# Pairwise bilinear products: two-tile loads of x from GpSimd in 16 KB rows, and W without its last zeros

## The chip, the cores and the metric

The kernel runs on one core of a Trainium2 chip. The metric is the device time of one launch in microseconds (us), lower is better. Before the change it was 1322.44 us, the median of 3 runs from 1320.73 to 1324.12. Everything is in 32-bit floats.

## The reference

For 4096 samples with 32 fields of 64 values each, every pair of fields i < j (496 pairs) has a matrix of its own. Field i is multiplied by the matrix, and the result elementwise by field j:

```python
i_idx, j_idx = np.triu_indices(32, k=1)        # 496 pairs
vi = inputs[:, i_idx, :]                       # (4096, 496, 64)
vj = inputs[:, j_idx, :]
vdotw = jnp.einsum('bpd,pde->bpe', vi, W)      # W: (496, 64, 64)
inter = vdotw * vj
return inter.reshape(4096, -1)                 # (4096, 31744)
```

The output has 520 MB, x (the inputs) 33.6 MB and W 8 MB. Nearly all that is moved is output.

## The kernel before

The samples are cut into 32 tiles of 128, one sample to a partition; a tile of x is 128 rows of 8 KB. For each tile TensorE transposes x in two halves, ScalarE copies the transposes to SBUF, TensorE multiplies them by W, and VectorE multiplies the products by x into a ring in SBUF. From the ring the tile goes out in four stores of 128 rows (30,208, 26,112, 31,488 and 39,168 bytes a row). The ring holds 28,160 columns, less than the 31,744 of a tile, so VectorE has to wait for stores. The first half of a tile's transposes is done within the last store group of the tile before it.

x has three slots in SBUF, and is loaded in the list that this function makes: load 0 is tile 0, load i is tiles 2i-1 and 2i in two slots side by side, and the last is tile 31 alone. Tile 2i-1 is always in slot 1; a load is written in the program at the start of tile 2i-2, and slot 1 is free when tile 2i-3 is done.

```python
DMA_ENGINES = 16
LIGHT = 4
LIGHT_TILES = [4, 6, 8, 10, 12, 14, 18, 20, 22, 24, 26, 28, 30]
PAIRS_FROM = [6, 8, 10, 12, 14, 0, 1]
HEAD = P // DMA_ENGINES        # 8
REST = HEAD // 2               # 4
PAD = 16

def x_slots(NT):
    loads = [[(0, 0)]]
    for t in range(1, NT, 2):
        if t + 1 == NT:
            loads.append([(t, 1)])
        elif loads[-1][-1] == (t - 1, 2):
            loads.append([(t + 1, 0), (t, 1)])
        else:
            loads.append([(t, 1), (t + 1, 2)])
    return loads
```

Most transfers are spread evenly over the 16 DMA engines, 8 rows to each. For some tiles GpSimd issues the load so that one engine (LIGHT) gets no rows of it: 120 rows go as 15 blocks of 8 rows to the 15 engines after it, and the other 8 rows as 2 blocks of 4 to two of the engines in the list PAIRS_FROM. The design rests on a cursor that moves round the engines with each DMA of GpSimd's; where it doesn't stand at the wanted engine, a small DMA of a few bytes (a nudge) moves it there. The blocks lie in DRAM with 16 elements of padding between them, so that a block stays a block.

```python
    def from_engine(e):
        nonlocal cursor
        k = (e - cursor) % DMA_ENGINES
        if k:
            nudge = nudges[e == LIGHT + 1]
            from_pool(
                nudge[:k].rearrange("p (h c) -> p h c", h=2)[:, :, :4],
                x[: k * 8].rearrange("(p h c) -> p h c", p=k, h=2),
            )
        cursor = e

    def load_beside(at, xt, lap):
        nonlocal cursor
        most = DMA_ENGINES - 1
        for e, k, rows, p in (
            (PAIRS_FROM[lap % len(PAIRS_FROM)], 2, REST, most * HEAD),
            (LIGHT + 1, most, HEAD, 0),
        ):
            from_engine(e)
            n = rows * F * D
            blocks = x[at : at + k * (n + PAD)].rearrange("(k c) -> k c", k=k)
            from_pool(xt[p : p + k * rows], blocks[:, :n])
            at += k * (n + PAD)
            cursor = (e + k) % DMA_ENGINES

    def load_x(load):
        at = sum(x_sizes[: x_loads.index(load)])
        parts = [[(t, s)] for t, s in load] if any(t in LIGHT_TILES for t, s in load) else [load]
        for part in parts:
            t, s = part[0]
            n = len(part) * F * D
            if t in LIGHT_TILES:
                load_beside(at, slot[t], LIGHT_TILES.index(t))
            else:
                nc.scalar.dma_start(
                    out=xbuf[:, s * F * D : s * F * D + n],
                    in_=x[at : at + P * n].rearrange("(p c) -> p c", p=P),
                )
            at += sum(tile_sizes[t] for t, s in part)
```

So 13 tiles come from GpSimd, 15 tiles singly from ScalarE's queue, and two loads (tiles 1 and 2, tiles 15 and 16) as pairs from ScalarE's queue in rows of 16 KB.

W lies in SBUF as 128 partitions: the upper 64 hold the matrices of even fields, the lower 64 those of odd ones. The odd fields have fewer pairs, so the lower half ends in 960 columns of zeros. W comes in five loads:

```python
    for g in LOADS:
        upto = woff[2 * g[-1]] + width[2 * g[-1]]
        nc.sync.dma_start(out=w_sb[:, done:upto], in_=w[:, done:upto])
        done = upto
```

Of the kernel before, what the change touches and what calls it, by code (L numbers as in the profile page):

```python
# [12 lines left out]
P = 128  # L13
# [10 lines left out]

DMA_ENGINES = 16
LIGHT = 4
LIGHT_TILES = [4, 6, 8, 10, 12, 14, 18, 20, 22, 24, 26, 28, 30]
PAIRS_FROM = [6, 8, 10, 12, 14, 0, 1]
HEAD = P // DMA_ENGINES
REST = HEAD // 2  # L30
PAD = 16
# [14 lines that stand above are left out]
# [3 lines left out]
def pair_bilinear_kernel(  # L49
# [32 lines left out]
    nc = tc.nc  # L82
    NT = out.shape[1] * 2 // (F * (F - 1) * D)
    NPR = F // 2

    width = [(F - 1 - i) * D for i in range(F)]
# [4 lines left out]
    woff = [i % 2 * D + sum(width[i % 2 : i : 2]) for i in range(F)]  # L91
# [13 lines left out]
    xbuf = const.tile([P, 3 * F * D], F32, tag="x", name="x")  # L105
    x_loads = x_slots(NT)
    pads = (DMA_ENGINES + 1) * PAD
    tile_sizes = [P * F * D + (pads if t in LIGHT_TILES else 0) for t in range(NT)]
    x_sizes = [sum(tile_sizes[t] for t, s in load) for load in x_loads]
    slot = {t: xbuf[:, ts(s, F * D)] for load in x_loads for t, s in load}  # L110

    nudges = [const.tile([DMA_ENGINES, 16], F32, tag=f"nudge{i}", name=f"nudge{i}") for i in range(2)]
# [2 lines left out]
    def from_pool(out, in_):  # L115

        tc.keep_in_program_order(nc.gpsimd.dma_start(out=out, in_=in_))  # L117

    def from_engine(e):

        nonlocal cursor
        k = (e - cursor) % DMA_ENGINES
        if k:
            nudge = nudges[e == LIGHT + 1]
            from_pool(
                nudge[:k].rearrange("p (h c) -> p h c", h=2)[:, :, :4],
                x[: k * 8].rearrange("(p h c) -> p h c", p=k, h=2),
            )
        cursor = e

    def load_beside(at, xt, lap):

        nonlocal cursor
        most = DMA_ENGINES - 1
        for e, k, rows, p in (
            (PAIRS_FROM[lap % len(PAIRS_FROM)], 2, REST, most * HEAD),
            (LIGHT + 1, most, HEAD, 0),
        ):
            from_engine(e)
            n = rows * F * D  # L140
            blocks = x[at : at + k * (n + PAD)].rearrange("(k c) -> k c", k=k)
            from_pool(xt[p : p + k * rows], blocks[:, :n])
            at += k * (n + PAD)
            cursor = (e + k) % DMA_ENGINES

    def load_x(load):

        at = sum(x_sizes[: x_loads.index(load)])
        parts = [[(t, s)] for t, s in load] if any(t in LIGHT_TILES for t, s in load) else [load]
        for part in parts:  # L150
            t, s = part[0]
            n = len(part) * F * D
            if t in LIGHT_TILES:
                load_beside(at, slot[t], LIGHT_TILES.index(t))
            else:
                nc.scalar.dma_start(
                    out=xbuf[:, s * F * D : s * F * D + n],
                    in_=x[at : at + P * n].rearrange("(p c) -> p c", p=P),
                )
            at += sum(tile_sizes[t] for t, s in part)  # L160

    pring = psum.tile([P, BANKS * BANK], F32, tag="pring", name="pring")
    bank = 0
# [21 lines left out]
    at = 0  # L185

    load_x(x_loads[0])
    w_sb = const.tile([P, sum(width[0::2])], F32, tag="w", name="w")
    done = 0
    for g in LOADS:  # L190

        upto = woff[2 * g[-1]] + width[2 * g[-1]]
        nc.sync.dma_start(out=w_sb[:, done:upto], in_=w[:, done:upto])
        done = upto

    transpose_x(slot[0], 0)
    for t in range(NT):
        xt = slot[t]
        for load in x_loads:
            if min(load)[0] == t + 1:  # L200
                load_x(load)
        for s, group in enumerate(STORES):
            if at + store_w[s] > RING:
                at = 0
# [3 lines left out]
            for p in group:  # L208
# [5 lines left out]
                for c1 in range(first, width[2 * p] + 1, BANK):  # L214
                    n = first if c1 == first else BANK
                    c0 = c1 - n
                    odd = width[2 * p + 1] and c1 > D
# [28 lines left out]
                out=out[:, t * cols + o0 : t * cols + o0 + store_w[s]], in_=osb  # L246
# [49 lines left out]
```

## Time and profile before

The profiled execution took 1321.16 us, with a span of 1319.0 us from its first to its last instruction and a mean granted TensorE clock of 0.970.

| | before |
|---|---|
| time, median of 3 | 1322.44 us |
| moved by DMA | 562.90 MB, mean 427 GB/s |
| HBM read, written | 41.95 MB, 520.09 MB |
| DMA packets | 25404 |
| store of 4896 KB, issue to landing | 17.7 us |
| x from ScalarE, 1024 KB, issue to landing | 18.7 us |
| x from GpSimd, 960 KB, issue to landing | 26.4 us |

Engines are TensorE (PE, and PEld for its weight loads), VectorE (DVE), ScalarE (ACT), GpSimd (POOL) and SyncE (SP), which issues the loads of W and the stores. A row of the queue table has packets, megabytes and the share of 16 engines' span that the packets took. q1 is SyncE's queue, q10 ScalarE's, q0 GpSimd's, q8 fetches instructions. A line such as "DVE ring L231 <- DMA out_dram<-ring" reads: VectorE at line 231, which writes the ring, waited for a store of the ring to DRAM; then the total in us, how often, and the longest wait. L181 is the transpose, L182 its copy, L221 the matmul, L231 and L239 VectorE's products, L156 ScalarE's load of x and L117 every DMA of GpSimd's. The table of stretches has, for each stretch of the span, the busy time of each engine, then the granted clock, the share of the 16 DMA engines' time that was busy (a packet is counted where it starts, so a short stretch can have over 1), and GB/s.

### The profile page before, as it was taken

What the parts mean: (1) busy time and instruction counts of PE and PEld (TensorE: products, weight loads), DVE (VectorE), ACT (ScalarE), POOL (GpSimd) and SP (SyncE); (2) the same over time, 40 slices, a digit from 0 to 9 for tenths busy, and PEclk for the clock granted to TensorE, in tenths of its full rate; (3) what the DMA queues carried; (4) which work ended last, traced back from release to release, by engine and by line L of the source; (5) the groups of instructions that cost most, each with busy time, mean ns of one, the idle gap of its engine ahead of it and who ended that gap; (6) DMA issues with size and microseconds to landing.
All of it is one profiled execution on the core that took longest, in us unless ns stands there. A gap on an engine that the chain in (4) does not pass through costs nothing.

```text
span 1319.0 us, 13176 instructions
## 1 busy us (share of the span) xinstructions
PE 1159.3 (88%) x5376; PEld 534.3 (41%) x5376; DVE 1182.1 (90%) x1376; ACT 66.1 (5%) x65; POOL 30.2 (2%) x58
## 2 busy tenths in 40 slices
PE   6998889889898998998999889888998989899893
PEld 3443344343444443443344444334443344344441
DVE  5998899989899998998999899889998989899894
ACT  1000000000000000000000000000000000000000
POOL 0000000000000000000000000000000000000000
PEclk9999999999999998998999989999999999999997
DMA  9999999999999999999999999999999999999998
GB/s 393 430 431 433 425 432 430 432 431 427 427 427 429 430 429 429 430 429 434 429 428 427 430 431 424 431 426 428 428 432 429 421 429 421 428 430 434 430 431 378
DMA packets 25404, 562.90 MB, mean 427 GB/s; under 512 B 4480, under 2 KB 4480, under 8 KB 4736
## 3 DMA queue, kind: packets, MB, share of 16 engines
q1 hardware_dynamic: 19152, 528.49, 93.5%
q10 hardware_dynamic: 2448, 19.92, 3.6%
q0 software_dynamic: 3744, 13.65, 2.5%
q8 instruction: 42, 0.69, 0.2%
q14 instruction: 18, 0.15, 0.0%
HBM read 41.95 MB, written 520.09 MB: 426 GB/s over the span
## 4 chain that ended last, share of the span: by engine, by line
DMA 50%; DVE 35%; issue 8%; PE 6%; DVEq 0%; ACT 0%
DMA out_dram<-ring 49%; DVE ring L231 30%; PE pring L221 6%; DVE ring L239 5%; DMA x<-in_x_dram 1%; DVEq L231 0%; PE pring L181 0%; ACT xT L182 0%; DVEq L292 0%; DVEq L239 0%
## 5 line engine op out<-in xcount | busy, mean ns | idle before, releaser
L221 PE MATMUL pring<-w,xT 64*128 64x512 f32 (+4 forms) x4864 | 1096.2, 561 | 132.1 <-DVE ring L231 111.1
L231 DVE TENSOR_TENSOR ring<-pring,x 128x1024 f32<-128x1024 f32 (+3 forms) x1056 | 1103.5, 1105 | 106.1 <-DMA out_dram<-ring 77.8
L221 PEld LDWEIGHTS pring<-w,xT 64*128 64x128 f32 x4864 | 478.8, 190 | 708.8 <-DVE ring L231 519.7
L182 ACT COPY xT<-pring 128x1024 f32<-128x1024 f32 x64 | 64.8, 1012 | 1208.9 <-PE pring L181 1208.9
L239 DVE TENSOR_TENSOR ring<-pring,x 128x64 f32<-128x64 f32 (+3 forms) x320 | 97.1, 352 | 13.6 <-DMA out_dram<-ring 13.6
L181 PEld LDWEIGHTS pring<-ident,x 128*128 128x128 f32 x512 | 55.5, 142 | 56.7 <-DVE ring L231 48.2
L181 PE MATMUL pring<-ident,x 128*128 128x128 f32 x512 | 70.8, 282 | 8.6 <-DMA x<-in_x_dram 8.5
L117 POOL DMA_DIRECT2D x<-in_x_dram x26 | 15.2, 585 | 1076.3 <-DVE ring L239 1076.1
L117 POOL DMA_DIRECT2D nudge<-in_x_dram x26 | 14.5, 559 | 0.3 <-issue 0.3
L182 ACT ACT_TABLE_LOAD x1 | 1.3, 1283 | 1.7 <-PEq L288 1.7
masks.py:199 POOL TENSOR_SCALAR_AFFINE_SELECT ident<-ident 128x128 f32<-128x128 f32 x1 | 0.3, 287 | 0.1
masks.py:197 POOL MEMSET ident<- 128x128 f32 x1 | 0.2, 204 | 0.3 <-POOLq L288 0.3
L288 POOL MEMSET const-float32-0.0<- 128x1 f32 x1 | 0.1, 98 | 0.2 <-issue 0.2
L288 POOL MEMSET const-bfloat16-1.0<- 128x1 bf16 x1 | 0.1, 101 | 0.0
L288 POOL MEMSET const-uint8-127<- 128x1 uint8 x1 | 0.1, 101 | 0.0
L288 POOL MEMSET const-float32-1.0<- 128x1 f32 x1 | 0.1, 98 | 0.0
## 6 DMA issues: line engine op xcount, KB each, us to landing
out_dram<-ring SPq DMA_DIRECT2D x32, 4896.0 KB, 17.7
out_dram<-ring SPq DMA_DIRECT2D x32, 3936.0 KB, 17.7
out_dram<-ring SPq DMA_DIRECT2D x32, 3776.0 KB, 19.7
out_dram<-ring SPq DMA_DIRECT2D x32, 3264.0 KB, 20.1
x<-in_x_dram ACTq DMA_DIRECT2D x15, 1024.0 KB, 18.7
x<-in_x_dram POOLq DMA_DIRECT2D x13, 960.0 KB, 26.4
x<-in_x_dram ACTq DMA_DIRECT2D x2, 2048.0 KB, 18.2
w<-in_w_dram SPq DMA_DIRECT2D x1, 2592.0 KB, 28.2
```

Source lines behind the costliest of these rows:

```text
L117: tc.keep_in_program_order(nc.gpsimd.dma_start(out=out, in_=in_))
L181: nc.tensor.transpose(pt[:, ts(c, P)], xt[:, ts(n * g + c, P)], ident)
L182: nc.scalar.copy(xT[:, ts(g, 2 * BANK)], pt)
L221: nc.tensor.matmul(pm[:, h * BANK : h * BANK + n], xT[h * D : (h + 1) * D, ts(p, P)], w_sb[h * D : (h + 1) * D, a : a + n], start=True, st ...
L231: nc.vector.tensor_tensor(runs(osb, o[0], o[1], n), runs(pm, 0, BANK, n), bass.AP(xj.tensor, xj.offset, [xj.ap[0], [0, 2], xj.ap[1]]), ALU ...
L239: nc.vector.tensor_tensor(osb[:, o[h] + h * D : o[h] + n], pm[:, h * (BANK + D) : h * BANK + n], xj[:, h * D :], ALU.mult,)
L288: nc = bacc.Bacc("TRN2", target_bir_lowering=False, num_devices=1)
```

## The change

GpSimd now brings whole loads of two tiles, in rows of 16 KB: six of them, loads 3, 5, 8, 10, 13 and 15 (tiles 5 and 6, 9 and 10, 15 and 16, 19 and 20, 25 and 26, 29 and 30). Twelve tiles instead of thirteen thus leave out the LIGHT engine. All other pairs come from ScalarE as one DMA of 16 KB rows. The last load of W is split into the columns in which both halves have data, and the last 960 columns of the upper half alone; the zeros are no longer moved. PAIRS_FROM is longer and starts elsewhere, and a nudge by one engine gets a form of its own, which doesn't occur with these lists. The aim is fewer and longer packets, fewer nudges and completions, less to move, and small blocks spread over more engines.

```diff
-LIGHT_TILES = [4, 6, 8, 10, 12, 14, 18, 20, 22, 24, 26, 28, 30]
-PAIRS_FROM = [6, 8, 10, 12, 14, 0, 1]
+LIGHT_LOADS = [3, 5, 8, 10, 13, 15]
+PAIRS_FROM = [5, 7, 9, 11, 13, 15, 1, 2, 0, 14, 12, 10, 8, 6]
 ...
-    def load_beside(at, xt, lap):
+    def load_beside(at, xt, n_row, lap):
 ...
-            n = rows * F * D
+            n = rows * n_row
 ...
     def load_x(load):
-        at = sum(x_sizes[: x_loads.index(load)])
-        parts = [[(t, s)] for t, s in load] if any(t in LIGHT_TILES for t, s in load) else [load]
-        for part in parts:
-            ... (each tile of a pair by itself, as above)
+        i = x_loads.index(load)
+        at = sum(x_sizes[:i])
+        n = len(load) * F * D
+        s = load[0][1]
+        xt = xbuf[:, s * F * D : s * F * D + n]
+        if i in LIGHT_LOADS:
+            load_beside(at, xt, n, LIGHT_LOADS.index(i))
+        else:
+            nc.scalar.dma_start(out=xt, in_=x[at : at + P * n].rearrange("(p c) -> p c", p=P))
 ...
         upto = woff[2 * g[-1]] + width[2 * g[-1]]
-        nc.sync.dma_start(out=w_sb[:, done:upto], in_=w[:, done:upto])
+        odd = woff[F - 1] + width[F - 1]
+        both = min(upto, odd)
+        nc.sync.dma_start(out=w_sb[:, done:both], in_=w[:, done:both])
+        if both < upto:
+            nc.sync.dma_start(out=w_sb[:D, both:upto], in_=w[:D, both:upto])
         done = upto
```

The order of x in DRAM is prepared to match: the rows of a GpSimd load hold both its tiles.

More of the change, by code (lines that the diff above doesn't have):

```diff
@@ L107, in pair_bilinear_kernel @@
     pads = (DMA_ENGINES + 1) * PAD
-    tile_sizes = [P * F * D + (pads if t in LIGHT_TILES else 0) for t in range(NT)]
-    x_sizes = [sum(tile_sizes[t] for t, s in load) for load in x_loads]
+    x_sizes = [
+        P * len(load) * F * D + (pads if i in LIGHT_LOADS else 0) for i, load in enumerate(x_loads)
+    ]
     slot = {t: xbuf[:, ts(s, F * D)] for load in x_loads for t, s in load}
@@ L124, in from_engine @@
             nudge = nudges[e == LIGHT + 1]
[L125 to L128, printed above, removed]
+            if k == 1:
+                from_pool(nudge[:3, :8], x[:64].rearrange("(g c) -> g c", g=2)[:, :12])
+            else:
+                from_pool(
+                    nudge[:k].rearrange("p (h c) -> p h c", h=2)[:, :, :4],
+                    x[: k * 8].rearrange("(p h c) -> p h c", p=k, h=2),
+                )
         cursor = e
-    def load_beside(at, xt, lap):
+    def load_beside(at, xt, n_row, lap):
         nonlocal cursor
@@ L146, in load_x @@
     def load_x(load):
-        at = sum(x_sizes[: x_loads.index(load)])
-        parts = [[(t, s)] for t, s in load] if any(t in LIGHT_TILES for t, s in load) else [load]
-        for part in parts:
[L151 to L160, printed above, removed]
+        i = x_loads.index(load)
[5 more added lines that the diff above has]
+            load_beside(at, xt, n, LIGHT_LOADS.index(i))
+        else:
+            nc.scalar.dma_start(out=xt, in_=x[at : at + P * n].rearrange("(p c) -> p c", p=P))
     pring = psum.tile([P, BANKS * BANK], F32, tag="pring", name="pring")
@@ L261 @@
     x = []
-    for load in x_slots(NT):
-        tiles = [t for t, _ in load]
-        if not any(t in LIGHT_TILES for t in tiles):
-            x.append(rows[:, tiles].ravel())
-            continue
-        for t in tiles:
-            if t in LIGHT_TILES:
-                k = (DMA_ENGINES - 1) * HEAD
-                for part in (
-                    rows[k:, t].reshape(2, REST * F * D),
-                    rows[:k, t].reshape(DMA_ENGINES - 1, HEAD * F * D),
-                ):
-                    x.append(np.pad(part, ((0, 0), (0, PAD))).ravel())
-            else:
-                x.append(rows[:, t].ravel())
+    for i, load in enumerate(x_slots(NT)):
+        of_load = rows[:, [t for t, _ in load]]
+        if i in LIGHT_LOADS:
+            k = (DMA_ENGINES - 1) * HEAD
+            for part in (of_load[k:].reshape(2, -1), of_load[:k].reshape(DMA_ENGINES - 1, -1)):
+                x.append(np.pad(part, ((0, 0), (0, PAD))).ravel())
+        else:
+            x.append(of_load.ravel())
     x = np.concatenate(x)
```

## The prediction

> **What bounds the kernel now.** I read the page from the top: busy shares first, then the slices, the queues and the chain, and after that the stretches at both ends.
>
> ```profile
> PE 1159.3 (88%) x5376; PEld 534.3 (41%) x5376; DVE 1182.1 (90%) x1376; ACT 66.1 (5%) x65; POOL 30.2 (2%) x58
> DMA  9999999999999999999999999999999999999998
> ...
> q1 hardware_dynamic: 19152, 528.49, 93.5%
> q10 hardware_dynamic: 2448, 19.92, 3.6%
> q0 software_dynamic: 3744, 13.65, 2.5%
> q8 instruction: 42, 0.69, 0.2%
> ...
> DMA 50%; DVE 35%; issue 8%; PE 6%; DVEq 0%; ACT 0%
> ```
>
> The queue shares add up to 99.8% of what 16 DMA engines can do in the span: the transfers are the bound, and the whole run is one long queue. VectorE at 90% comes second, and the waits say that it is held by the stores, which free the ring:
>
> ```profile
> DVE ring L231 <- DMA out_dram<-ring: 77.8, 43, 6.1
> DVE ring L231 <- PE pring L221: 17.4, 8, 13.5
> DVE ring L239 <- DMA out_dram<-ring: 13.6, 6, 2.9
> PE pring L181 <- DMA x<-in_x_dram: 8.5, 1, 8.5
> ```
>
> The last of these lines matters later: the matrix engine waits once for x, at the start, and never again. The table of stretches shows full DMA in the middle and where the run is not full:
>
> ```profile
> 0.00:20.00 20.00, 10.36 (x42) 5.57 (x44) 5.89 (x6) 2.29 (x2) 1.39 (x7) 1.00 0.92 377
> 160.00:320.00 160.00, 143.42 (x670) 66.13 (x668) 146.35 (x171) 8.10 (x8) 4.49 (x8) 0.98 1.00 430
> 1104.00:1107.00 3.00, 3.00 (x15) 2.09 (x15) 3.00 (x8) 0.00 (x0) 1.33 (x3) 1.00 0.97 417
> 1301.00:1310.00 9.00, 0.00 (x0) 0.00 (x0) 0.83 (x4) 0.00 (x0) 0.00 (x0) 0.55 1.01 437
> 1310.00:1319.00 9.00, 0.00 (x0) 0.00 (x0) 0.00 (x0) 0.00 (x0) 0.00 (x0) 0.50 0.55 239
> ```
>
> Columns are busy time of PE, PEld, DVE, ACT and POOL, then the granted clock, the DMA share and GB/s. I also added up the packet records of the trace (start, duration, bytes; they carry no engine number). A packet starts some 3.5 ns before the one ahead of it on its engine ends; with that taken off, the 16 engines are busy for 20,993 engine-us, or 1312.0 us each. The rest of the 1319.0 us is 2.0 us until the first packets move, 1.5 us of engines run dry at the ends of some tiles (the stretch at 1104 is one), and about 3.5 us at the end, of which the last 16 completions, spread over 3.26 us, are the larger part. So a change in transfers is worth its sum over the 16 engines, divided by 16, plus what it does to the balance between them.
>
> The same records give the price of a row: 309 ns for 8 KB, 611 for 16 KB, 771 for a 20,736-byte row of W, 1448 for a 39,168-byte store row, and 9 for a 4-byte completion. So one 16 KB row in place of two of 8 KB saves 2 x 309 - 611 = 7 ns in the records, and 3.5 ns of engine time once each overlap is taken off. From 39,168 and 8,192 bytes the slope is 36.8 ns per 1000 bytes, the fixed part about 8 ns.
>
> One engine is slow: of the 4096 rows of each kind of store, 202, 222, 242 and 416 are 12 to 60 ns over the usual duration, near a sixteenth (256), by 29, 31, 36 and 32 ns on average. With 8 rows of each kind in a tile, that engine needs about 1.0 us more per tile, 33 us in 32 tiles. This is the engine that the GpSimd loads spare; followed back from the end it finishes second to last, 0.11 us before the last, at 2.1 us after the mean of the sixteen.
>
> **What the Trainium skill says.** All on its page "DMA: Bandwidth & Descriptors". "Why a DMA increments its semaphore by 16 and not by 1": a GpSimd DMA goes to k consecutive engines from a round-robin cursor, and all 16 post a completion. The second half agrees with the trace: the 52 GpSimd DMAs left 1664 four-byte packets, 32 each, where one from a hardware queue leaves 16. "Queues, rings and completion order": an engine takes its queues in turn, packet by packet. This agrees: the rows of a GpSimd load, 8 of 309 ns on an engine, are spread over 20 to 23 us between store rows. "Why small descriptors are slow (HBM only)": each packet has a fixed cost; here about 8 ns, so longer rows can bring little at these sizes. "Where 436 GB/s comes from": the ceiling is 435 GB/s; the full stretches move 430, so there is no rate left to gain.
>
> **The change part by part,** in engine time of one DMA engine (records less 3.5 ns).
>
> 1. W's last load. 8 rows of 771 become 8 of 16,896 bytes (estimate from the slope and the fixed part: 630) and 4 of 3840 bytes (149), since 64 partitions over 16 engines are 4 each, plus one completion: 8 x 767.5 = 6140 before, 8 x 626.5 + 4 x 145.5 + 5.5 = 5600 after. Saves 0.54 us on every engine. It is on the path: loads are queued from 2 us on and stores follow without a gap.
> 2. ScalarE's loads. Before, 15 single tiles and 2 double ones: 8 x (15 x 305.5 + 2 x 607.5) = 46.38 us. After, 2 single and 9 double: 8 x (2 x 305.5 + 9 x 607.5) = 48.63. Adds 2.25 us on every engine, the spared one too.
> 3. GpSimd's large parts. On the 15 others, 13 x 8 x 305.5 = 31.77 us become 6 x 8 x 607.5 = 29.16: saves 2.61.
> 4. GpSimd's small parts. 26 shares of four 8 KB rows become 12 of four 16 KB rows, 2.43 us each against 1.22. By the list of starts, engines 6 to 15 and 0 had two shares and now have one (no change), engine 1 had three and now none (-3.67), 2 had one and now none (-1.22), 5 had none and now one (+2.43), 3 none and none. All together -2.5 us.
> 5. Completions and nudges. 28 GpSimd DMAs fewer, 2 completions on each engine: 28 x 2 x 5.5 ns = 0.31 us; 6 loads of ScalarE fewer: 0.03; nudge packets 416 to 188: 0.08. Saves 0.42.
>
> Sum for most engines: -0.54 + 2.25 - 2.61 - 0.42 = -1.3 us. For the spared engine: -0.54 + 2.25 - 0.42 = +1.3. The mean over 16, with part 4: (15 x -1.32 - 2.5 + 1.3) / 16 = -1.3 us. GpSimd's 28 fewer issues of 0.56 to 0.59 us and ScalarE's six cost nothing now: both engines idle over 90%.
>
> **The end.** The spared engine was ahead of the mean at most tile ends of the first 420 us (0.5 to 2 us, by its long rows) and fell behind only after its last relief, the load issued at 1106.8 us. In the new kernel the last relief is tiles 29 and 30, issued when tile 27 is done, near 1146: some 40 us later, worth about 1 us less of lag at 1.0 us per 41 us tile. That eats most of its +1.3. The engine with three small shares loses them. I take 0.2 us off the tail. With the mean this gives -1.5 us: 1322.4 - 1.5 = 1320.9.
>
> **Rivals.**
>
> First, x arrives too late. The double load waits for both slots, the second of which comes free when the tile two before is done. ScalarE's load at that same moment shows the time left:
>
> ```profile
> 175.03 0.36 ACTq L156 DMA_DIRECT2D x<-in_x_dram  x1
> 186.29 1.01 ACT L182 COPY xT<-pring 128x1024 f32<-128x1024 f32 x1 [19.96 <-PE pring L181]
> 205.67 1.01 ACT L182 COPY xT<-pring 128x1024 f32<-128x1024 f32 x1 [18.37 <-PE pring L181]
> ...
> x<-in_x_dram POOLq DMA_DIRECT2D x13, 960.0 KB, 26.4
> ```
>
> The second copy is of the new tile; its transposes begin 1.2 us earlier, 29.5 us after the release. At the six places the window is 29.5, 31.5, 33.0, 32.3, 31.7 and 29.9 us. A large GpSimd load lands 26.4 us after its issue, which comes 1.1 us after the release; 8 rows longer by 0.30 us make it 29.9. Two of six touch the matrix engine by under a microsecond. For it: tile ends are where engines run dry, so a late store is not wholly absorbed. Against it: x's extra 2.4 us also delays the stores of that tile, and the window with them. If landing takes 5 us more than that, six stalls cost up to 20 us: 1340.
>
> Second, the balance. Relief comes in six lumps of 4.9 us, not thirteen of 2.4, with up to 165 us between them, in which the slow engine falls back some 4 us. It may run dry after a lump and hold the ring later. In the whole run the dry time is 1.5 us per engine; doubling or tripling it gives +1.5 to +3: 1322.5 to 1324.
>
> Third, the spared engine's +1.3 us alone sets the end, as it was nearly last: 1323.7.
>
> Fourth, tiles without any x load become VectorE's. Against it: tile 13 has none, and from 539.4 to 575.7 it took 36.3 us at a DMA share of 1.01, so VectorE still keeps the engines full.
>
> **Range and chances.** Everything counted is within 3 us of 0, about 0.2%, and the three runs of before already differ by 3.4 us. I predict 1320.9 us, 1318.3 to 1324.2. Faster by over 2% (26 us) is ruled out by full engines and equal bytes: 0.01. Slower by over 2% needs late loads at all six places, or rows cut smaller than 16 KB together with stalls: 0.02. Within 2%: 0.97.
>
> **What would show it.** The queues should read 19232 packets for stores and W, 1584 for ScalarE, 1724 for GpSimd, with 16 KB rows in both x queues; HBM reads fall by 0.25 MB from 41.95. Engine time per engine should be near 1310.7 us. A wait of L181 on x beyond the first one would show the first rival; DMA shares under 0.9 at tile ends near 220 to 300 or 1030 to 1110 us the second; a last completion well after the others, on long rows, the third. I am wrong if the time leaves the range, or if it is in the range while dry time and tail moved by more than the 1.3 us of work.

## The result and the profile after

The changed kernel takes 1328.24 us (median of 6 runs, 1326.43 to 1331.11), against 1323.28 us for the kernel before (6 runs beside it, 1319.82 to 1325.67). The ratio is 1.0041, with a 95% interval of 1.0021 to 1.0061: slower by 0.4%, or 5 us, where the prediction had 1.5 us less. It lies outside the range of 1318.3 to 1324.2.

The page of the changed kernel, in the parts shown of the one before:

```profile
PE 1159.8 (87%) x5376; PEld 539.9 (41%) x5376; DVE 1182.1 (89%) x1376; ACT 66.1 (5%) x65; POOL 14.4 (1%) x30
...
DMA  9999999999999999999999999999999999999998
...
q1 hardware_dynamic: 19232, 528.25, 93.2%
q10 hardware_dynamic: 1584, 20.97, 3.7%
q0 software_dynamic: 1728, 12.59, 2.3%
q8 instruction: 42, 0.69, 0.2%
...
DMA 42%; DVE 39%; issue 10%; PE 7%; DVEq 0%; POOL 0%; ACT 0%
```

All the counting came out: 19232, 1584 and (but for 4) 1724 packets, and fewer bytes. The shares of the queues still add up to 99.4%. Nothing here says where 10 us of span have gone (1319.0 to 1329.3 in the two profiled runs; the changed kernel's was the slowest of its six). The share of VectorE's steps in the chain has grown from 35% to 39%, that of DMA fallen from 50% to 42%: a hint that VectorE more often comes last.

The waits of the changed kernel:

```profile
DVE ring L235 <- DMA out_dram<-ring: 87.4, 35, 6.5
PE pring L181 <- DMA x<-in_x_dram: 19.8, 5, 8.5
DVE ring L235 <- PE pring L225: 18.0, 11, 13.5
DVE ring L243 <- DMA out_dram<-ring: 12.8, 3, 5.9
```

The transposes now wait for x five times, not once: late x, the first rival, is there, with 11.3 us in four waits. Whether it costs anything has to be tried.

The table of stretches tells more than the page. Of the changed kernel: the same stretches as before, then one dry tile end, and two of GpSimd's loads with one of ScalarE's for comparison (columns as before; the last two are the DMA share and GB/s):

```profile
0.00:20.00 20.00, 10.39 (x44) 5.63 (x44) 5.93 (x6) 2.29 (x2) 1.39 (x7) 1.00 0.93 380
160.00:320.00 160.00, 142.49 (x666) 66.35 (x662) 145.19 (x170) 8.10 (x8) 2.25 (x4) 0.97 1.00 426
1311.00:1320.00 9.00, 0.00 (x0) 0.00 (x0) 0.63 (x4) 0.00 (x0) 0.00 (x0) 0.56 1.00 431
1320.00:1329.30 9.30, 0.00 (x0) 0.00 (x0) 0.00 (x0) 0.00 (x0) 0.00 (x0) 0.50 0.56 240
...
702.00:708.00 6.00, 5.77 (x31) 3.62 (x29) 6.00 (x13) 0.00 (x0) 0.00 (x0) 1.00 0.76 329
...
585.00:610.00 25.00, 20.58 (x88) 7.68 (x88) 21.37 (x23) 1.01 (x1) 0.00 (x0) 1.00 0.99 403
749.00:774.00 25.00, 19.76 (x86) 7.29 (x84) 19.18 (x20) 1.01 (x1) 0.00 (x0) 1.00 0.98 397
...
257.00:274.00 17.00, 14.22 (x68) 5.94 (x64) 13.39 (x14) 1.01 (x1) 0.00 (x0) 1.00 1.01 434
```

Of the kernel before, two of GpSimd's loads in rows of 8 KB:

```profile
139.00:161.00 22.00, 20.24 (x90) 7.53 (x88) 19.71 (x20) 1.01 (x1) 0.00 (x0) 1.00 0.98 417
300.00:322.00 22.00, 20.46 (x90) 7.59 (x88) 21.08 (x23) 1.01 (x1) 0.00 (x0) 1.00 1.00 423
```

Two things are to be seen. While a double load of GpSimd's runs, the engines are as busy as ever (0.98 and 0.99) and move 397 and 403 GB/s; beside a ScalarE load of the same rows of 16 KB they move 434, and beside the old loads of GpSimd's 417 and 423. A full share at a lower rate means that the packets themselves got longer. And at some tile ends the share drops: 0.76 over 6 us.

Rates of such short stretches are rough, for a packet is counted where it starts. With 2 or 3 us more at each end, the first of the changed kernel's two loads and the first of the old kernel's read:

```profile
583.00:612.00 29.00, 23.66 (x109) 9.47 (x108) 24.45 (x26) 1.11 (x2) 0.00 (x0) 1.00 1.01 414
```

```profile
136.00:163.00 27.00, 23.29 (x103) 8.89 (x101) 22.98 (x25) 1.01 (x1) 0.23 (x1) 1.00 1.01 431
```

ScalarE's load reads 423 GB/s from 254 to 276 us. So the changed kernel's loads still stand out, but less, and the old ones no longer do.

Both can be summed over the packet records. *Excess* is the duration of packets over the usual one for their size (8 KB 309 ns, 16 KB 611 ns, the store rows 968, 1119, 1166 and 1448 ns), for all x and store packets from 1 us before to 1 us after a load's rows. It leaves out store rows that start still earlier and are under way when the load arrives. Counted from 2.6 us before the first row, a double load of ScalarE's in the changed kernel (without the one at the start of the run) has 7.0 engine-us, two thirds of it on eight or nine such rows, each longer by about one x row; a single load of ScalarE's in the kernel before has 2.7. GpSimd's loads change little by it, from 4.3 to 4.8 and from 20.3 to 21.1. *Dry* is the time in which an engine has no packet, between 40 us and 7 us before the end, per engine.

| profiled run | span | busy per engine | dry per engine | excess per GpSimd load |
|---|---|---|---|---|
| before | 1319.0 us | 1312.0 us | 1.5 us | 4.3 engine-us, one tile |
| changed | 1329.3 us | 1316.9 us | 6.8 us | 20.3 engine-us, two tiles |

Busy without all excess was 1312.0 - 8.9 = 1303.1 us before and 1316.9 - 15.0 = 1301.9 after: the work fell by the 1.2 us that were counted on. The excess rose by 6.1 us per engine, of which 4.1 lie beside GpSimd's loads and about 1 beside ScalarE's, early rows counted; the dry time rose by 5.3. These are sums for the slowest of the six runs; the four other kernels with 16 KB rows in blocks from GpSimd, in the table of all sums below, have less of both. Of the excess of a GpSimd load, 2.9 of 20.3 engine-us lie on its own rows and 17.3 on the store rows beside them. Most of it falls in the second and third quarters of a load, from the moment the large part's rows begin: the fifteen engines take their first long row within 0.9 to 2.4 us of each other. Per load 15 store rows are lengthened by 0.45 us or more (about an x row) and 36 by 0.06 to 0.25 us.

### The profile page after: what moved, and what is told of

It reads as the page before. It is cut to its first block, busy times and chain, and to the rows that moved or that the text cites. A ratio compares the mean times of both kernels' runs of the same rounds, so it can differ in the third digit from the quotient of the medians.

```text
span 1329.3 us, 13115 instructions
## 1 busy us (share of the span) xinstructions
PE 1159.8 (87%) x5376; PEld 539.9 (41%) x5376; DVE 1182.1 (89%) x1376; ACT 66.1 (5%) x65; POOL 14.4 (1%) x30
## 3 DMA queue, kind: packets, MB, share of 16 engines
q1 hardware_dynamic: 19232, 528.25, 93.2%
q10 hardware_dynamic: 1584, 20.97, 3.7%
## 4 chain that ended last, share of the span: by engine, by line
DMA 42%; DVE 39%; issue 10%; PE 7%; DVEq 0%; POOL 0%; ACT 0%
DMA out_dram<-ring 39%; DVE ring L235 34%; PE pring L225 7%; DVE ring L243 5%; DMA x<-in_x_dram 3%; PE pring L181 0%; DVEq L235 0%; ACT xT L182 0%; POOL x L118 0%; POOL nudge L118 0%; DVEq L289 0%; DVEq L243 0%
## 5 line engine op out<-in xcount | busy, mean ns | idle before, releaser
L118 POOL DMA_DIRECT2D x<-in_x_dram x12 | 7.0, 586 | 1139.0 <-DVE ring L243 894.9
L118 POOL DMA_DIRECT2D nudge<-in_x_dram x12 | 6.8, 565 | 0.3 <-issue 0.3
## 6 DMA issues: line engine op xcount, KB each, us to landing
x<-in_x_dram POOLq DMA_DIRECT2D x6, 1920.0 KB, 30.5
```

## The experiments

The theory of *long rows*: long rows of a GpSimd load lengthen the store packets beside them, and the engines, slowed unevenly, run dry. Its rivals are *bunching* (x comes two tiles at a time, late or in bursts, and VectorE falls behind) and *lumps* (the slow engine gets its relief in six lumps and the engines lose step). The letters in the quoted expectations stand each for what that text says. Ratios are to the kernel before, run beside each.

**W alone.** `w_only`: the kernel before with W's last load as in the change.

```diff
-        nc.sync.dma_start(out=w_sb[:, done:upto], in_=w[:, done:upto])
+        both = min(upto, odd)
+        nc.sync.dma_start(out=w_sb[:, done:both], in_=w[:, done:both])
+        if both < upto:
+            nc.sync.dma_start(out=w_sb[:D, both:upto], in_=w[:D, both:upto])
```

> The kernel before with only the change to W's last load. The sum of engine time: 0.54 us less per engine, so 1322.7 us against 1323.3, if W's zeros are on the path as predicted. A theory that the split of W costs something at the start (rows of 3840 bytes were slow there, 205 ns on average against 149) expects 0 to +1 us. Neither explains the +5 us of the whole change.

1320.99 us, ratio 0.9989 (0.9982 to 0.9997). Faster by about 1.4 us, 0.4 to 2.4 by the interval; the 0.54 expected lies in it. In the records the rows of W's last load took 0.74 us less per engine than before (0.53 in the changed kernel). So the loss is in x, and is 5.5 to 6.5 us rather than 5.

**The blocks' spacing.** `pad4k`: the changed kernel with more room between blocks in DRAM.

```diff
-PAD = 16
+PAD = 1040
```

> The changed kernel with 4160 bytes instead of 64 between the blocks of a GpSimd load in DRAM, nothing else. Theory A (blocks of 128 KB plus 64 bytes make the 15 engines read DRAM in step and get in each other's way): the rows' excess over their usual duration in a GpSimd load falls from about 20 engine-us to 4 to 9, engine time falls by about 4 us per engine, and the time to 1324. Theory B (long rows themselves, or the bunching of x, cost it): the excess stays near 20 per load and the time near 1328.

1327.5 us, ratio 1.0036 (1.0021 to 1.0051), excess 18.3 per load. The spacing does not matter.

**GpSimd's rows.** `pool8k`: the same pairs of tiles at the same moment, each as two loads in rows of 8 KB, the tile in slot 1 first (the list PAIRS_FROM was set to 6, 8, 10, 12, 14, 0).

```diff
-            load_beside(at, xt, n, LIGHT_LOADS.index(i))
+            for j, (t, s) in enumerate(by_tile(load)):
+                load_beside(at, slot[t], F * D, 2 * LIGHT_LOADS.index(i) + j)
+                at += P * F * D + pads
```

> The changed kernel, but each GpSimd load is two loads of one tile in rows of 8 KB, issued one after the other at the same moment as the double one. The bunching of x and the lumps of relief stay, the rows and blocks are those of before. If rows or blocks of GpSimd's loads are the cause: excess per pair of tiles back at about 9 engine-us, engine time 4 us less, time 1324 or a little above. If bunching and lumps are: dry time stays near 6 us per engine and the time near 1328. If both: about 1326.

1322.57 us, ratio 1.0000 (0.9992 to 1.0009): against 1.0041, this one edit gives back most of the loss. Excess is 9.8 engine-us per pair of tiles, busy time 1312.5, dry time 2.3 us. One of its pairs, and the tile end that was dry in the changed kernel, in the table of stretches:

```profile
580.00:622.00 42.00, 37.03 (x176) 17.63 (x172) 38.23 (x45) 2.02 (x2) 1.70 (x3) 0.96 1.01 431
...
702.00:708.00 6.00, 5.59 (x30) 2.62 (x26) 6.00 (x6) 0.00 (x0) 0.00 (x0) 1.00 1.00 432
```

431 GB/s through the load where the changed kernel had 403 in nearly the same place, and no gap near 705 us. Its six pairs ran at 421 to 431 GB/s, the six of the changed kernel at 396 to 419.

**ScalarE's rows.** `act8k`: the changed kernel with ScalarE's pairs as single tiles.

```diff
-            nc.scalar.dma_start(out=xt, in_=x[at : at + P * n].rearrange("(p c) -> p c", p=P))
+            for t, s in load:
+                nc.scalar.dma_start(out=slot[t], in_=x[at : at + P * F * D].rearrange("(p c) -> p c", p=P))
+                at += P * F * D
```

> The changed kernel, but ScalarE's nine double loads are single tiles in rows of 8 KB, the first of which goes out some 9 us ahead of the second. GpSimd's loads stay double. If the bunching of x by ScalarE makes the engines run dry (the dry ends of tiles 10, 12, 16, 20, 22 follow a ScalarE load): dry time falls from 6.8 us per engine to 3 or less, time about 1325. If GpSimd's loads are the whole cause: no change, 1328.

1327.32 us, ratio 1.0034 (1.0021 to 1.0048); dry time 3.7 us in the profiled run, excess still 17.2. ScalarE's bursts are not what costs most of the time; a microsecond or two could hide in the intervals. Dry time is the least steady of the sums: it fell here without the time following by more than the noise.

**Late x.** `late_half`: the changed kernel, with the next tile's transposes later.

```diff
-FIRST_HALF_AT, SECOND_HALF_AT = 9, 3
+FIRST_HALF_AT, SECOND_HALF_AT = 11, 3
```

> The changed kernel, but the first half of the next tile's transposes comes before pair 11 instead of pair 9 of the last group, some 3 us later, with loads and rows as they are. The waits of the transposes on x beyond the one at the start, 11.3 us in four places, should all but go. If late x costs the time: 1324 to 1326. If the slow rows and the spread of the engines cost it: the waits go and the time stays at 1327 to 1329.

1327.08 us, ratio 1.0041 (1.0028 to 1.0054). Its waits on x:

```profile
PE pring L181 <- DMA x<-in_x_dram: 8.5, 1, 8.5
```

The four new waits are gone and the ratio is what it was: late x is not the cause. A cost of a microsecond or two could hide in the intervals.

**One DMA in short rows.** `rows8k_one`: the large part as one DMA of 240 rows.

```diff
+            if k == most:
+                src = x[at : at + k * n].rearrange("(t p c) -> p t c", t=2, c=F * D)
+                from_pool(xt[p : p + k * rows].rearrange("p (t c) -> p t c", t=2), src)
+            else:
 ...          (the two lines as they were)
```

> The changed kernel, but the large part of a GpSimd load is one DMA of 240 rows of 8 KB (both tiles of a partition one after the other) instead of 120 rows of 16 KB; its small part keeps rows of 16 KB. Theory A (the length of the row: an engine that takes store rows and x rows in turn lengthens its store rows more, the longer the x row) expects what two separate loads of 8 KB rows gave: excess near 10 engine-us per load and a time of 1322 to 1324. Theory B (so many bytes of one DMA to one engine, whatever the rows) expects an excess near 20 and 1328.

1353.1 us, ratio 1.0238 (1.0221 to 1.0255). The excess is 10.1 per load, as the theory of long rows has it, and busy time 1312.5. The small part and its list of engines are those of the changed kernel, so it is the large part's rows that made the excess. But the time is far worse than either theory said, and the profile shows why. Its wait on x, and three stretches around its first GpSimd load:

```profile
PE pring L185 <- DMA x<-in_x_dram: 65.5, 7, 10.9
```

```profile
177.00:210.00 33.00, 21.74 (x96) 7.99 (x92) 25.45 (x26) 1.01 (x1) 0.00 (x0) 0.92 1.00 417
210.00:216.00 6.00, 4.88 (x22) 3.45 (x24) 1.07 (x2) 1.01 (x1) 0.00 (x0) 0.57 1.02 441
216.00:224.00 8.00, 7.78 (x41) 4.48 (x39) 7.87 (x14) 0.00 (x0) 0.00 (x0) 1.00 0.30 124
```

Sixteen short rows take turns with sixteen store rows where eight long ones took turns with eight, so the load lands 37.4 us after its issue, not 30.5. The transposes wait for it six times (57 us beyond the start), VectorE has nothing to do, and 6 us later the engines have run out of stores: a share of 0.30. Dry time is 33.2 us per engine. So this is what late x looks like when it matters: waits of 9.5 us cost 5 us each (30.5 us over pool8k, in six), where those of 1.4 to 4.1 us in the changed kernel cost nothing that shows, presumably as there were still stores in the queue. Short rows and a close deadline don't go together in one DMA.

**Queue or blocks.** Two kernels, of which there is one run each. `pool_plain` sends GpSimd's double loads as plain ones over all 16 engines; `act_blocks` sends the blocks from ScalarE's queue.

```diff
-            load_beside(at, xt, n, LIGHT_LOADS.index(i))
+            from_pool(xt, x[at : at + P * n].rearrange("(p c) -> p c", p=P))
```

> The changed kernel, but the six GpSimd loads are plain ones: 128 rows of 16 KB, 8 rows to each of 16 engines, no small part, no nudges. The slow engine isn't spared, so the time itself says little: with 29 us more work on it than on average, 1340 to 1350. What counts is the excess of the rows while such a load runs. If the cause is that GpSimd's queue carries the rows: near 20 engine-us per load as in the changed kernel. If it is the blocks (8 neighbouring partitions to one engine, 15 engines in step): near ScalarE's, 1.5 to 3.5.

```diff
-        tc.keep_in_program_order(nc.gpsimd.dma_start(out=out, in_=in_))
+        nc.scalar.dma_start(out=out, in_=in_)
 ...
-            from_engine(e)
```

> The changed kernel, but ScalarE's queue issues the same 120 and 8 rows in the same blocks, with no nudges. Fifteen engines still get 8 rows of 16 KB of neighbouring partitions, though not the same fifteen, so the slow engine isn't spared: 1335 to 1350. If the blocks are the cause: excess near 20 engine-us per load. If GpSimd's queue is: 1.5 to 5.

1337.91 and 1340.43 us; in neither is the slow engine spared, so these times say little. Excess: 12.1 engine-us per plain GpSimd load, 31.7 per load of blocks from ScalarE, where plain double loads from ScalarE have 1.0 in the first and about 1 in the second. With the store rows under way at the start of a load, as above, it is 13.0, 32.8, and for ScalarE's plain loads 8.0 and 6.9. Of the second kernel, one load of blocks and one plain one, both of ScalarE's:

```profile
342.00:364.00 22.00, 15.13 (x64) 6.73 (x66) 15.09 (x16) 1.01 (x1) 0.00 (x0) 0.80 1.00 393
...
257.00:273.00 16.00, 13.69 (x65) 5.71 (x62) 12.95 (x14) 1.01 (x1) 0.00 (x0) 1.00 1.02 438
```

The same queue, the same row length, 393 against 438 GB/s (398 against 430 with 2.6 us more at the start). GpSimd's queue is not needed for it: blocks make long rows costly from ScalarE's. But a plain GpSimd load has more than a plain one of ScalarE's too, 13.0 against 8.0; the records name no engine and no partition, so whether its rows are dealt out in blocks too isn't seen.

**DRAM or SBUF.** `interleave`: blocks as in the changed kernel in SBUF, but in DRAM the 15 engines read neighbouring rows at the same time.

```diff
+            if k == most:
+                src = x[at : at + k * n].rearrange("(r k c) -> k r c", k=k, r=rows)
+            else:
 ...          (the blocks as they were)
```

> The changed kernel, but the 120 rows of a GpSimd load lie in DRAM so that the 15 engines read neighbouring rows of 16 KB at the same time, and an engine's eight rows are 240 KB apart, instead of eight rows in one run of 128 KB. Partitions and engines in SBUF are the same. If the DRAM side of the blocks makes rows slow: excess falls from 20 engine-us per load to 12 or less, and the time to 1325. If the SBUF side does: 18 to 22 and 1328.

1326.73 us, ratio 1.0034 (1.0022 to 1.0046); excess 17.3 per load. Three runs with the same loads as the changed kernel have 20.3, 17.2 and 15.5, so 17.3 is no change: the order in DRAM hardly counts. The SBUF side of the blocks, 8 neighbouring partitions to an engine, is what suggests itself next. It was not tried by itself.

**Bunching or lumps.** With W's change, pool8k's pairs were still some 1.5 us behind w_only. `all8k_spread` takes the bunching away: every tile a load of its own in 8 KB rows, that with the earlier free slot first. The edit is shown against pool8k.

```diff
-    return sorted(load, key=lambda ts: ts[1] != 1)
+    return sorted(load, key=lambda ts: ts[1] == 1)
 ...          (and ScalarE's pairs as single tiles, in this order)
```

> GpSimd brings the same six pairs of tiles as in the changed kernel, but every tile is a load of its own in rows of 8 KB, and of each pair the tile whose slot is free earlier goes first; ScalarE's pairs likewise. W as in the changed kernel. Against GpSimd's pairs in 8 KB rows back to back (1322.6) it takes away the bunching of x, and keeps the relief of the slow engine in six lumps. If bunching is what is left between that kernel and the one with only W's change (1321.0): 1321. If the lumps are: 1322.6.

1323.02 us, ratio 1.0002 (0.9994 to 1.0010). Bunching is not the rest. `w_12` is w_only with twelve tiles from GpSimd, nearly evenly spread:

```diff
-LIGHT_TILES = [4, 6, 8, 10, 12, 14, 18, 20, 22, 24, 26, 28, 30]
+LIGHT_TILES = [4, 6, 8, 10, 12, 14, 18, 20, 22, 24, 26, 30]
```

> The kernel with only W's change, with twelve tiles from GpSimd instead of thirteen: tile 28 comes from ScalarE. Rows of 8 KB, one tile at a time, relief nearly even. If the 1.5 us between that kernel (0.9989 of before) and the two with twelve tiles in six pairs in rows of 8 KB (1.0000 and 1.0002) come from less relief of the slow engine: ratio 1.000. If they come from its coming in six lumps: 0.999, as with thirteen.

1320.28 us, ratio 0.9988 (0.9980 to 0.9997). One relief less is not the rest either. What differs is that the relief comes in six pairs, the first of them later: the theory of lumps, worth about 1.4 us, by elimination and not shown by itself. The small parts also go to partly other engines, and with these intervals the 1.4 us are only just clear of noise.

**Shorter rows still.** If long rows are bad, the loads of the kernel before may gain from rows of 4 KB: they have over 80 us to land in. `w_rows4k` is w_only with the large part of GpSimd's single tiles in 240 rows:

```diff
+            if k == most:
+                src = x[at : at + k * n].rearrange("(h p c) -> p h c", h=2, c=F * D // 2)
+                from_pool(xt[p : p + k * rows].rearrange("p (h c) -> p h c", h=2), src)
+            else:
 ...          (the two lines as they were)
```

> The kernel before with W's change, and the large part of GpSimd's single-tile loads in 240 rows of 4 KB instead of 120 of 8 KB. These loads have over 80 us to land in, so their being longer costs no wait. If excess follows the length of the row: it falls from 3.4 engine-us per load (44 in all) to about 2, 1.2 us less per engine, less 0.4 for the added rows: 1320. If it doesn't: 1321.5.

1318.29 us, ratio 0.9965 (0.9952 to 0.9978): the fastest of all, faster than both kernels. But not for the reason expected: excess is 3.3 per load against 3.4, and busy time 1310.2 against 1310.5. Dry time is 0.4 us against 1.2. Why it is faster stays open. `w_rows2k` writes the same with `h=4`, in 480 rows of 2 KB:

> The kernel with W's change and the large part of GpSimd's single-tile loads in 480 rows of 2 KB. If shorter rows of a GpSimd load go on letting the engines keep step: dry time under 0.5 us per engine and about 1318, as with rows of 4 KB, or 1 us less. The added rows cost 3 packets of about 4 to 8 ns on each engine for each of 8 rows of 13 loads, 1.2 to 2.5 us against rows of 8 KB; if that is all they do, 1322.

1319.88 us, ratio 0.9984 (0.9976 to 0.9993). By the queue table it moves the same packets; first of w_rows4k, then of w_rows2k:

```profile
q0 software_dynamic: 5408, 13.65, 2.6%
```

```profile
q0 software_dynamic: 5408, 13.65, 2.6%
```

Both have 3120 packets of 4096 bytes; rows of 2 KB show no packets of their own. So little is learned of 2 KB, and the two ratios may well be of one thing, between 0.9965 and 0.9984. Short rows in loads with time to spare do no harm; with W's change they beat both the kernel before and the changed one; that they beat w_only's 0.9989 rests on the first alone.

All sums, from one profiled run of each:

| kernel | ratio (interval) | busy | dry | excess per GpSimd load |
|---|---|---|---|---|
| changed | 1.0041 (1.0021 to 1.0061) | 1316.9 | 6.8 | 20.3, two tiles |
| pad4k | 1.0036 (1.0021 to 1.0051) | 1315.8 | 4.2 | 18.3, two tiles |
| act8k | 1.0034 (1.0021 to 1.0048) | 1314.5 | 3.7 | 17.2, two tiles |
| late_half | 1.0041 (1.0028 to 1.0054) | 1315.0 | 3.6 | 15.5, two tiles |
| interleave | 1.0034 (1.0022 to 1.0046) | 1315.3 | 5.2 | 17.3, two tiles |
| pool8k | 1.0000 (0.9992 to 1.0009) | 1312.5 | 2.3 | 9.8, two tiles |
| all8k_spread | 1.0002 (0.9994 to 1.0010) | 1312.2 | 2.4 | 4.8, one tile |
| w_only | 0.9989 (0.9982 to 0.9997) | 1310.5 | 1.2 | 3.4, one tile |
| w_12 | 0.9988 (0.9980 to 0.9997) | 1311.2 | 2.4 | 3.8, one tile |
| w_rows2k | 0.9984 (0.9976 to 0.9993) | 1311.9 | 1.6 | 4.3, one tile |
| w_rows4k | 0.9965 (0.9952 to 0.9978) | 1310.2 | 0.4 | 3.3, one tile |

The five kernels with GpSimd rows of 16 KB in blocks are all 0.3 to 0.4% slower than before; the six without are all level or faster. Left out are rows8k_one, which waits for x, and the two in which the slow engine isn't spared.

## Why the prediction was wrong

- *What bounds the kernel* was right: with every engine full, time is the sum of packets over 16, plus dry time, plus the two ends. Busy time came to 1316.9 us where 1310.7 was expected.
- *W's last load* (0.54 us saved) was right: 0.53 us in its rows in the changed kernel and 0.74 in w_only, whose interval for the time holds the 0.54.
- *ScalarE's loads*: the rows kept to their 611 ns. What they do to the store rows was left out here too, 7.0 engine-us for a double load against 2.7 for a single one, in all about 1 us per engine in the records. In the time it doesn't show: act8k, which undoes the double loads, has much the same.
- *GpSimd's large parts* is the step that failed. It took 611 ns a row from ScalarE's plain loads and found 2.61 us saved. The rows themselves nearly kept to that price (634 ns on average), but they lengthen the store packets around them: 6 loads of 20.3 engine-us against 13 of 4.3 are 66 engine-us more, 4.1 us per engine, in this run, and 3 us with the mean of the three runs with such loads (17.7). Where the sum had -2.61 it should have had at least +0.5. pool8k, with the same bytes in rows of 8 KB, gave most of the loss back. The trace of before had a slight hint in its packet records, 4.8 engine-us for a GpSimd load beside 2.7 for one of ScalarE's, and I priced rows without looking at what they do to the others. Its GB/s gave none that is safe: 417 from 139 to 161 us, 431 from 136 to 163.
- *Small parts, completions and nudges* and the mean of -1.3 us: the work less excess fell by 1.2 us.
- *First rival, late x*: the waits came, at four places and not two, and of 1.4 to 4.1 us where the text had "under a microsecond", for the loads landed 30.5 us after their issue and not the 28.8 that its sum comes to. They cost nothing that shows (late_half). The guess that 5 us more of landing would cost up to 20 us was right in kind: rows8k_one landed 6.9 us later and lost 25 us against the changed kernel.
- *Second rival, the balance*: the dry time rose to 6.8 us, 4.5 times what it was, against "doubling or tripling". The share fell to 0.76 near 705 us and 0.80 near 1033, the second of these where the text looked for it. Most of the dry time went with the long rows (2.3 us in pool8k), but the other kernels with such rows have 3.6 to 5.2, so how much is their consequence is not settled; for the lumps about 1.4 us remain.
- *Third rival, the spared engine sets the end*: no. The last engine to finish in the changed kernel had usual durations in all rows of its last store and ended 3 us after the first, as before (3.05 against 3.26 us). The 0.2 us taken off the tail can't be told from noise.
- *Fourth rival, tiles without x*: ScalarE's bursts cost nothing that shows in the time (act8k), as the text said.

## What to carry to other kernels

A packet's own duration isn't its price when the engines are full: sum what all packets beside that kind of load take over their usual durations, with those under way when it arrives, and so price the neighbours too. GB/s at equal DMA share points the same way, but the ends of a stretch of 20 us shifted it by up to 14 GB/s here. Rows of 16 KB dealt out in blocks of eight neighbouring partitions lengthened the packets around them about twice as much as rows of 8 KB did for the same bytes, while a plain load of ScalarE's with 16 KB rows had 7.0 engine-us against 5.3 for two with 8 KB rows; short rows were safe as long as the load had time, for each of them takes turns with a store row. A wait that a change brought cost time that shows only where the queue behind it ran dry before it ended.

## What the runs showed of the hardware that was not expected

- The same 16 KB rows moved at 438 GB/s beside stores in a plain load from ScalarE's queue, and at 393 in blocks from the same queue (430 and 398 with 2.6 us more at the start). Why is open: not the spacing and hardly the order in DRAM; the SBUF side was not tried.
- Store rows that are under way when a plain load of ScalarE's with 16 KB rows arrives take about one such row longer: eight or nine of them per load in the changed kernel, by some 0.55 us. They start up to 2.1 us before the load's first row.
- GpSimd's loads with a large part of 480 rows of 2 KB show the same 3120 packets of 4096 bytes in 13 loads as with 240 rows of 4 KB.
- Towards the end of the kernel before, the store rows of the slow engine took up to 52 ns more than usual until about the last VectorE instruction, and all rows of the last store the usual 1448 ns. The changed kernel ends alike. Whether the compute engines are the reason was not tried.
